# A two-layer graph network kernel: gather in plain f32, one summed row-norm operand, other first loads, another order of the last pair

## The chip, the cores and the metric

The kernel runs on one core of a Trainium2 chip. The metric is the device time of one execution in microseconds (us), 1934.1 as the median of three runs (1933.42 to 1934.23). In the profile PE is TensorE (matmuls), PEld its loading of weights, DVE is VectorE, ACT is ScalarE, POOL is GpSimd and SP is SyncE, which here only starts transfers.

## The reference

There are 64 graphs of 256 nodes with 512 features, one adjacency matrix of 256 x 256 zeros and ones for all, and two layers:

```python
# layer 0
h = relu(layernorm(x))
q, k, v = h @ Wq.T, h @ Wk.T, h @ Wv.T
rel = adj.T * (q @ k.T)
rel = rel / norm(rel, axis=2)           # length of each row
x = x + rel @ v
# layer 1
h = relu(layernorm(x))
x = x + (adj @ h) @ weight + bias
```

All of it is float32.

## The kernel before

**Tiling.** The graphs are taken two at a time, as 32 pairs. A pair is a tile `x` of 128 partitions by 2 graphs by 2 halves of the nodes by 512 features (1 MB). Layer 0 folds Wq and Wk into one matrix, `m_sb`, made at the start (L346 to L355), so that only `g` (`project_g`) and `v` (`project_v`) are computed per pair. These two and layer 1's product with `weight` (`mix`) use a Winograd form of the 2 x 2 block product: seven block products instead of eight (`winograd`, L137), each of four matmuls, accumulated in three PSUM banks `bank_a`, `bank_c` and `bank_b` and taken out between them by ACT copies (first write) or DVE additions. Their left sums come from `left_sums` on DVE.

**Stages of pair i.** `ln0` normalizes x and applies the relu (statistics on DVE, the relu as four ACT instructions, L200). `transposes` turns h on TensorE through one PSUM bank, copied out by ACT. `scores` makes rel (L260), multiplies it with adj on DVE and squares it on ACT into `sq` (L265). `attend` computes rel @ v (L275) and the row norms: for each 128 rows two matmuls of `sq`, one for each half of the other node index, with a column of ones, added up in the bank `pn` (L285). ACT and DVE then turn `pn` into 1/norm (L290, L291) and DVE adds to x (L293). `ln1` normalizes the new x, applies the relu, and adds the bias to x on POOL (L309). `gather` is adj @ h2 (L323). `gather_sums` and `mix` finish layer 1, and the pair goes out in one transfer from POOL (L343).

**Two forms of gather.** At the start the kernel looks at the low 12 bits of all entries of adj (L372 to L383). If any is set, it runs the loop over the pairs with `gather` as plain f32 matmuls. If none is set (zeros and ones have none), it runs a second copy of the loop in which h2 is written as a sum of two fp32r terms `h2s`: ACT casts each of the four chunks (L204), DVE subtracts the cast from the original (L205), and `gather` multiplies both terms with `adjt_r`, an fp32r copy of adj transposed. A value read into registers and a branch (L421 to L426) choose the copy; nothing of a branch mixes with what stands before it.

**Order.** The loop over pairs is software-pipelined by hand: scores(i), sums of gather(i-1), transposes(i+1), mix(i-1), attend(i), project_g(i+1), ln1(i), project_v(i+1), ln0(i+2), gather(i). The order of the text is a rank. The framework's planner places each engine's instructions ahead of time by that rank and by its own estimate of when each is ready, adds the waits, and hands out buffers; each engine then works through its list in that fixed order. So an instruction of lower rank may be placed ahead of one of higher rank where the planner sees a gap.

**Loads.** SP starts the loads of x, three pairs ahead (L80). The first x has a buffer of its own, the others share four. ACT starts Wq, Wk and Wv in this order, POOL starts adj, `weight` and the bias.

Of the kernel before, what the change touches and what calls it, by code (L numbers as in the profile page):

```python
# [8 lines left out]

F32 = mybir.dt.float32  # L10
F32R = mybir.dt.float32r
I32 = mybir.dt.int32
AF = mybir.ActivationFunctionType
ALU = mybir.AluOpType
EPS = 1e-5
# [3 lines left out]
def kernel(  # L19
# [22 lines left out]

    nc = tc.nc
    P = 128
    B, N, D = x.shape
# [11 lines left out]
    outs = out.rearrange("(i b) (c p) d -> i p b c d", b=NB, p=P)  # L65

    const = ctx.enter_context(tc.tile_pool(name="const", bufs=1))
    xpool = ctx.enter_context(tc.tile_pool(name="xpool", bufs=4))
    work = ctx.enter_context(tc.tile_pool(name="work", bufs=1))
    small = ctx.enter_context(tc.tile_pool(name="small", bufs=3))  # L70
    ps_t = ctx.enter_context(tc.tile_pool(name="ps_t", bufs=1, space=bass.MemoryType.PSUM))
# [3 lines left out]
    X, H, HT, HS, G, V, R, H2, Y, YS = ({} for _ in range(10))  # L75

    def load(i):
        pool, tag = (const, "x_first") if i == 0 else (xpool, "x")
        X[i] = pool.tile([P, NB, NC, D], F32, tag=tag, name=f"x_{i}")
        nc.sync.dma_start(out=X[i], in_=xs[i])  # L80


    load(0)
    ident = const.tile([P, P], F32, name="ident")
    make_identity(nc, ident)
    ones = const.tile([P, 1], F32, name="ones")
    nc.gpsimd.memset(ones, 1.0)

    wq_sb = work.tile([P, DC, D], F32, tag="g", name="wq_sb")
    wk_sb = work.tile([P, DC, D], F32, tag="v", name="wk_sb")  # L90
    wv_sb = work.tile([P, DC, D], F32, tag="yt", name="wv_sb")
    nc.scalar.dma_start(out=wq_sb, in_=wq.rearrange("(c p) d -> p c d", p=P))
    nc.scalar.dma_start(out=wk_sb, in_=wk.rearrange("(c p) d -> p c d", p=P))
    nc.scalar.dma_start(out=wv_sb, in_=wv.rearrange("(c p) d -> p c d", p=P))
    adj_sb = const.tile([P, NC, N], F32, name="adj_sb")
    nc.gpsimd.dma_start(out=adj_sb, in_=adj.rearrange("(c p) n -> p c n", p=P))
    w_sb = const.tile([P, DC, D], F32, name="w_sb")
    nc.gpsimd.dma_start(out=w_sb, in_=weight.rearrange("(c p) d -> p c d", p=P))
    bias_bc = const.tile([P, D], F32, name="bias_bc")
    nc.gpsimd.dma_start(  # L100
        out=bias_bc, in_=bass.AP(tensor=bias.tensor, offset=bias.offset, ap=[[0, P], [1, D]])
# [78 lines left out]
        return product  # L180


    def norm_relu(dst, src, split=None):

        st = small.tile([P, TC, 6], F32, tag="st", name="st")
        mv = small.tile([P, TC, 2], F32, tag="mv", name="mv")
        rs = small.tile([P, TC], F32, tag="rs", name="rs")  # L190
        nb = small.tile([P, TC], F32, tag="nb", name="nb")
        for c in range(TC):
            nc.vector.bn_stats(st[:, c, :], src[:, c, :])  # L193
            nc.vector.bn_aggr(mv[:, c, :], st[:, c, :])  # L194
        nc.vector.tensor_scalar(rs, mv[:, :, 1], 0.0, EPS, op0=ALU.max, op1=ALU.add)
        nc.scalar.activation(rs, rs, AF.Sqrt)
        nc.vector.reciprocal(rs, rs)
        nc.vector.scalar_tensor_tensor(nb, mv[:, :, 0], -1.0, rs, op0=ALU.mult, op1=ALU.mult)
        for c in range(TC):
            nc.scalar.activation(  # L200
                dst[:, c, :], src[:, c, :], AF.Relu, bias=nb[:, c : c + 1], scale=rs[:, c : c + 1]
            )
            if split is not None:
                nc.scalar.copy(split[:, 0, c, :], dst[:, c, :])  # L204
                nc.vector.tensor_sub(split[:, 1, c, :], dst[:, c, :], split[:, 0, c, :].bitcast(F32))  # L205


    def ln0(i):
        pool, tag = (const, "h_first") if i == 0 else (work, "h")
        H[i] = pool.tile([P, TC, D], F32, tag=tag, name=f"h_{i}")  # L210
        norm_relu(H[i], flat(X[i]))

    def transposes(i):
        h = H.pop(i)
# [37 lines left out]
    def scores(i):  # L252
        ht, g = HT.pop(i), G.pop(i).rearrange("p e h (b n) -> p e h b n", b=NB)
        rel = work.tile([P, NB, NC, N], F32, tag="rel", name=f"rel_{i}")
        sq = work.tile([P, NB, NC, N], F32, tag="sq", name=f"sq_{i}")
        for b in range(NB):
            pm = ps_m.tile([P, NC, N], F32, tag="pm", name="prel")
            for m in range(NC):
                for e in range(DC):
                    nc.tensor.matmul(  # L260
                        pm[:, m, :], ht[:, e, m, ts(b, P)], g[:, e, :, b, :],
                        start=(e == 0), stop=(e == DC - 1),
                    )
            nc.vector.tensor_mul(rel[:, b], pm, adj_sb)  # L264
            nc.scalar.activation(sq[:, b], rel[:, b], AF.Square)  # L265
        R[i] = (rel, sq)

    def attend(i):
        (rel, sq), v, xt = R.pop(i), flat(V.pop(i)), flat(X[i])
        pu = []  # L270
        for b in range(NB):
            for n in range(NC):
# [8 lines left out]
        for b in range(NB):  # L281
            for n in range(NC):
                c = b * NC + n
                for m in range(NC):
                    nc.tensor.matmul(  # L285
                        pn[:, c : c + 1], sq[:, b, m, ts(n, P)], ones,
                        start=(m == 0), stop=(m == NC - 1),
                    )
        rn = small.tile([P, TC], F32, tag="rn", name="rn")
        nc.scalar.activation(rn, pn, AF.Sqrt)  # L290
        nc.vector.reciprocal(rn, rn)  # L291
# [4 lines left out]
            )  # L296


    def ln1(i, exact):
        h2 = work.tile([P, TC, D], F32, tag="h2", name=f"h2_{i}")  # L300
        xt = flat(X[i])
        if exact:
            H2[i] = work.tile([P, 2, TC, D], F32R, tag="h2s", name=f"h2s_{i}")
            norm_relu(h2, xt, split=H2[i])
        else:
            H2[i] = h2
            norm_relu(h2, xt)
        for c in range(TC):
            nc.gpsimd.tensor_tensor(xt[:, c, :], xt[:, c, :], bias_bc, ALU.add)  # L309

    def gather(i, exact):
        h2 = H2.pop(i)
        if exact:
            terms = [(h2[:, s], adjt_r[:, m, :], m) for m in range(NC) for s in range(2)]
        else:
            terms = [(h2, adjt_sb[:, m, :], m) for m in range(NC)]
        Y[i] = work.tile([P, DC, NC, NB, P], F32, tag="yt", name=f"yt_{i}")
        for b in range(NB):
            for d0 in range(0, DC, 2):
                pm = ps_m.tile([P, 2, N], F32, tag="pm", name="py")  # L320
                for d in range(2):
                    for n, (left, right, m) in enumerate(terms):
                        nc.tensor.matmul(  # L323
                            pm[:, d, :], left[:, b * NC + m, ts(d0 + d, P)], right,
                            start=(n == 0), stop=(n == len(terms) - 1),
                        )
                nc.scalar.copy(
                    Y[i][:, d0 : d0 + 2, :, b, :], pm.rearrange("p d (h n) -> p d h n", h=NC)
                )
        Y[i] = Y[i].rearrange("p d h b n -> p d h (b n)")  # L330
# [4 lines left out]
    def mix(i):  # L335
# [4 lines left out]
            nc.vector.tensor_add(dst, bank.rearrange("p (b e) -> p b e", b=NB), dst)  # L340

        winograd(product_weights_moving(left_operands(Y.pop(i), YS.pop(i)), w_right), take)
        nc.gpsimd.dma_start(out=outs[i], in_=xt)  # L343


    m_sb = const.tile([P, DC, D], F32, name="m_sb")  # L346
# [18 lines left out]
    for m in range(NC):  # L365
# [3 lines left out]
    w_right = right_operands(w_sb, "w")  # L369


    adjt_r = const.tile([P, NC, N], F32R, name="adjt_r")  # L372
    nc.vector.tensor_copy(adjt_r, adjt_sb)
    low = const.tile([P, NC * N], I32, name="low")
    nc.vector.tensor_single_scalar(
        low, adj_sb.rearrange("p c n -> p (c n)").bitcast(I32), 0xFFF, op=ALU.bitwise_and
    )
    low_max = const.tile([P, 1], F32, name="low_max")
    nc.vector.tensor_reduce(low_max, low, axis=mybir.AxisListType.X, op=ALU.max)
    pf = ps_m.tile([P, 512], F32, tag="pm", name="pf")  # L380
    nc.tensor.matmul(pf[0:1, 0:1], low_max, ones, start=True, stop=True)
    low_any = const.tile([1, 1], I32, name="low_any")
    nc.vector.tensor_copy(low_any, pf[0:1, 0:1])  # L383


    ln0(0)

    def pairs(exact):
        for j in (1, 2):
            if j < NP:  # L390
                load(j)
        transposes(0)
        project_g(0)
        project_v(0)
        if NP > 1:
            ln0(1)
        for i in range(NP):
            nxt = i + 1 < NP
            if i + 3 < NP:
                load(i + 3)  # L400
            scores(i)
            if i > 0:
                gather_sums(i - 1)
            if nxt:
                transposes(i + 1)
            if i > 0:
                mix(i - 1)
            attend(i)
            if nxt:
                project_g(i + 1)  # L410
            ln1(i, exact)
            if nxt:
                project_v(i + 1)
            if i + 2 < NP:
                ln0(i + 2)
            gather(i, exact)
        gather_sums(NP - 1)
        mix(NP - 1)

    first = X[0], H[0]  # L420
    inexact = nc.values_load(low_any[0:1, 0:1], min_val=0, max_val=P * 0xFFF)  # L421
    with tc.If(inexact > 0) as either:
        pairs(False)
    X[0], H[0] = first
    with either.Else():
        pairs(True)  # L426


# [26 lines left out]
```

## Time and profile before

| | us |
|---|---|
| median of three runs | 1934.1 |
| the profiled execution's own time | 1934.1 |
| its span, first to last recorded event | 1932.3 |
| PE busy | 1876.4 |
| PEld busy | 1540.2 |
| DVE busy | 952.9 |
| ACT busy | 599.9 |
| POOL busy | 230.6 |

A line of the costliest groups gives the line of the source, the engine and operation, what is written from what, shapes and type, and the number of instructions; after the bar the busy time of the group in us and the mean of one in ns; after the second bar how long the engine was idle just before them, and what ended most of that. A line of the order of time gives start and length in us, engine, line, operation, and in brackets a wait ahead of it. Matmuls are pipelined and their ends are modelled, so the recorded lengths of neighbours overlap; the distance between the starts of two stages is the safer measure. In the chain of waits, "issue" is time in which the engine waited for nothing that the profile shows.

### The profile page before, as it was taken

How to read it: one execution, taken by the hardware profiler on the slowest of the kernel's cores; microseconds unless marked ns; L12 is line 12 of the kernel's file. 1: busy time of each engine (PE TensorE's matmuls, PEld its weight loads, DVE VectorE, ACT ScalarE, POOL GpSimd, SP SyncE). 2: the span in 40 equal slices, each digit the busy share in tenths (PEclk: the TensorE clock that was granted, in tenths of full speed). 3: DMA queues.
4: the chain of work that ended last, by engine and by line, in shares of the span. 5: the costliest groups of instructions: out<-in, count | busy, mean ns of one | idle time of the engine just before them, and what ended most of it. 6: DMA issues, size and time to landing. Idle time of an engine off the chain costs nothing.

```text
span 1932.3 us, 21628 instructions
## 1 busy us (share of the span) xinstructions
PE 1876.4 (97%) x9014; PEld 1540.2 (80%) x9014; DVE 952.9 (49%) x1744; ACT 599.9 (31%) x1066; POOL 230.6 (12%) x170
## 2 busy tenths in 40 slices
PE   4999999999999999999999999999999999999996
PEld 2788878888878888878888888888888888788885
DVE  2355554455554454554455554454554454554444
ACT  2233332233332333332333322333322333322321
POOL 0011110011110111110111110111110111110111
PEclk8999999999999999999999999999999999999998
DMA  5000111101111101111101111001111001110001
GB/s 174 35 13 10 44 44 44 44 1 44 44 44 44 44 1 44 44 44 44 37 8 44 44 44 44 24 21 44 44 44 44 22 23 44 44 44 23 10 13 44
DMA packets 27721, 73.28 MB, mean 38 GB/s; under 512 B 1120, under 2 KB 1120, under 8 KB 27616
## 3 DMA queue, kind: packets, MB, share of 16 engines
q1 hardware_dynamic: 16896, 33.56, 5.3%
q0 software_dynamic: 9136, 35.13, 4.8%
q10 hardware_dynamic: 1584, 3.15, 0.4%
q8 instruction: 72, 1.18, 0.2%
q14 instruction: 33, 0.27, 0.0%
HBM read 38.27 MB, written 33.55 MB: 37 GB/s over the span
## 4 chain that ended last, share of the span: by engine, by line
PE 66%; DVE 21%; ACT 11%; DMA 1%; issue 1%; DVEq 0%; POOLq 0%; ACTq 0%
PE bank_a L175 18%; PE prel L260 11%; PE pu L275 11%; DVE st L193 7%; ACT h L200 7%; PE py L323 6%; PE bank_c L175 6%; PE bank_b L175 5%; DVE h2s L205 4%; DVE x L293 4%; PE pt L220 3%; PE pn L285 3%; ACT h2s L204 2%; DVE g L235 2%; DVE mv L194 1%; PE pw L350 1%
## 5 line engine op out<-in xcount | busy, mean ns | idle before, releaser
L309 POOL TENSOR_TENSOR x<-x,bias_bc 128x512 f32<-128x512 f32 x128 | 203.0, 1614 | 630.8 <-ACT h L200 617.2
L200 ACT ACTIVATE h<-x,nb,rs 128x512 f32<-128x512 f32 x256 | 194.3, 807 | 105.8 <-DVE mv L194 55.0
L260 PE MATMUL prel<-g,ht 128*128 128x256 f32 x1024 | 226.2, 379 | 0.0
L275 PE MATMUL pu<-v,rel 128*128 128x512 f32 x512 | 225.4, 592 | 0.0
L260 PEld LDWEIGHTS prel<-g,ht 128*128 128x128 f32 x1024 | 192.1, 190 | 24.9
L205 DVE TENSOR_TENSOR h2s<-h,h2s 128x512 fp32r<-128x512 f32 x128 | 165.7, 1334 | 46.8 <-ACT h2s L204 46.7
L275 PEld LDWEIGHTS pu<-v,rel 128*128 128x128 f32 x512 | 97.0, 190 | 107.3 <-issue 105.7
L290 ACT ACTIVATE rn<-pn 128x4 f32<-128x4 f32 x32 | 5.6, 174 | 548.4 <-PE pn L285 548.4
L193 DVE BATCH_NORM_STATS2 st<-x 128x6 f32<-128x512 f32 x256 | 167.1, 665 | 0.8 <-DMA x<-in_x_dram 0.8
L343 POOL DMA_DIRECT2D out_dram<-x x32 | 24.7, 772 | 1064.6 <-DVE x L340 928.8
L323 PE MATMUL py<-adjt_r,h2s 128*128 128x256 f32 x1024 | 133.9, 289 | 9.7 <-ACT h2s L204 9.0
L175 PE MATMUL bank_a<-wv_t,hs 128*128 128x256 f32 x512 | 127.2, 391 | 12.6 <-ACT v L246 12.6
L323 PEld LDWEIGHTS py<-adjt_r,h2s 128*128 128x128 f32 x1024 | 126.5, 192 | 12.2 <-ACT h2s L204 9.1
L291 DVE RECIPROCAL rn<-rn 128x4 f32<-128x4 f32 x32 | 5.7, 178 | 253.2 <-ACT rn L290 253.2
L175 PEld LDWEIGHTS bank_a<-wv_t,hs 128*128 128x128 f32 x512 | 92.3, 189 | 45.5 <-ACT v L246 35.4
L340 DVE TENSOR_TENSOR x<-bank_a,x 128x512 f32<-128x512 f32 x128 | 88.0, 687 | 69.3 <-PE bank_a L175 69.3
L163 PE MATMUL bank_a<-hs,m_t 128*128 128x256 f32 x512 | 121.0, 379 | 0.0
L175 PE MATMUL bank_a<-w_t,ys 128*128 128x256 f32 x512 | 121.0, 379 | 0.0
L223 ACT COPY ht<-pt 128x512 f32<-128x512 f32 x128 | 75.0, 586 | 143.4 <-PE pt L220 143.4
L163 PEld LDWEIGHTS bank_a<-hs,m_t 128*128 128x128 f32 x512 | 97.2, 190 | 13.3 <-ACT g L233 0.2
L175 PEld LDWEIGHTS bank_a<-w_t,ys 128*128 128x128 f32 x512 | 97.3, 190 | 13.2
L264 DVE TENSOR_TENSOR rel<-prel,adj_sb 128x512 f32<-128x512 f32 x64 | 44.3, 692 | 114.3 <-PE prel L260 114.3
(101 smaller groups left out, 2830.3 us busy)
## 6 DMA issues: line engine op xcount, KB each, us to landing
x<-in_x_dram SPq DMA_DIRECT2D x32, 1024.0 KB, 5.5
out_dram<-x POOLq DMA_DIRECT2D x32, 1024.0 KB, 4.7
wq_sb<-in_L_gnn_Wq_dram ACTq DMA_DIRECT2D x1, 1024.0 KB, 11.7
wk_sb<-in_L_gnn_Wk_dram ACTq DMA_DIRECT2D x1, 1024.0 KB, 15.1
wv_sb<-in_L_gnn_Wv_dram ACTq DMA_DIRECT2D x1, 1024.0 KB, 17.1
w_sb<-in_L_gnn_weight_dram POOLq DMA_DIRECT2D x1, 1024.0 KB, 10.7
adj_sb<-in_adj_dram POOLq DMA_DIRECT2D x1, 256.0 KB, 7.4
bias_bc<-in_L_gnn_bias_dram POOLq DMA_DIRECT2D x1, 256.0 KB, 11.0
```

What stands on the lines that cost most here:

```text
L163: nc.tensor.matmul(bank[:, e * HT_ : (e + 1) * HT_], right[n][:, d, ts(e, P)], left[n][:, d, :], start=(start and e == 0 and d == 0), stop ...
L175: nc.tensor.matmul(bank[:, b * HD : (b + 1) * HD], left[n][:, d, ts(b, P)], right[n][:, d, :], start=(start and b == 0 and d == 0), stop=( ...
L193: nc.vector.bn_stats(st[:, c, :], src[:, c, :])
L200: nc.scalar.activation(dst[:, c, :], src[:, c, :], AF.Relu, bias=nb[:, c : c + 1], scale=rs[:, c : c + 1])
L205: nc.vector.tensor_sub(split[:, 1, c, :], dst[:, c, :], split[:, 0, c, :].bitcast(F32))
L223: nc.scalar.copy(HT[i][:, d].rearrange("p h t -> p (h t)"), pt)
L260: nc.tensor.matmul(pm[:, m, :], ht[:, e, m, ts(b, P)], g[:, e, :, b, :], start=(e == 0), stop=(e == DC - 1),)
L275: nc.tensor.matmul(pm[:, :D], rel[:, b, m, ts(n, P)], v[:, b * NC + m, :], start=(m == 0), stop=(m == NC - 1),)
L293: nc.vector.scalar_tensor_tensor(xt[:, c, :], pu[c][:, :D], rn[:, c : c + 1], xt[:, c, :], op0=ALU.mult, op1=ALU.add,)
L309: nc.gpsimd.tensor_tensor(xt[:, c, :], xt[:, c, :], bias_bc, ALU.add)
L323: nc.tensor.matmul(pm[:, d, :], left[:, b * NC + m, ts(d0 + d, P)], right, start=(n == 0), stop=(n == len(terms) - 1),)
L340: nc.vector.tensor_add(dst, bank.rearrange("p (b e) -> p b e", b=NB), dst)
```

## The change

- The look at adj's low bits, the branch and the copy of the loop with fp32r terms go. One loop remains, with `gather` as f32 matmuls of h2 and `adjt_sb`.
- In `scores`, POOL adds the squares of the two halves into a new tile `sqs`; in `attend` one matmul for each 128 rows takes the place of two.
- First loads: Wq goes first on SP, then x_0, behind it the other x; ACT starts Wk, Wv and `weight`; POOL starts adj and the bias. x_0 comes from the shared buffers, now five, and h_0 from the shared one.
- `norm_relu` is split into `norm` (statistics, scale and shift) and `relu`. In layer 1 `norm` keeps its place ahead of project_v(i+1), and `relu` with the bias additions comes after it.
- In the last pair, mix(30) comes after attend(31) and norm(31), ahead of the relu. The last pair's output is started on SP in two transfers, one for each half of the nodes.

```diff
-    xpool = ctx.enter_context(tc.tile_pool(name="xpool", bufs=4))
+    xpool = ctx.enter_context(tc.tile_pool(name="xpool", bufs=5))
...
+    nc.sync.dma_start(out=wq_sb, in_=wq.rearrange("(c p) d -> p c d", p=P))
+    nc.scalar.dma_start(out=wk_sb, in_=wk.rearrange("(c p) d -> p c d", p=P))
     load(0)
+    nc.scalar.dma_start(out=wv_sb, in_=wv.rearrange("(c p) d -> p c d", p=P))
...
-    nc.gpsimd.dma_start(out=w_sb, in_=weight.rearrange("(c p) d -> p c d", p=P))
+    nc.scalar.dma_start(out=w_sb, in_=weight.rearrange("(c p) d -> p c d", p=P))
...
+        sqs = work.tile([P, NB, N], F32, tag="sqs", name=f"sqs_{i}")
+        nc.gpsimd.tensor_tensor(sqs, sq[:, :, 0], sq[:, :, 1], ALU.add)
+        R[i] = (rel, sqs)
...
-                for m in range(NC):
-                    nc.tensor.matmul(
-                        pn[:, c : c + 1], sq[:, b, m, ts(n, P)], ones,
-                        start=(m == 0), stop=(m == NC - 1),
-                    )
+                nc.tensor.matmul(pn[:, c : c + 1], sqs[:, b, ts(n, P)], ones, start=True, stop=True)
...
-                    for n, (left, right, m) in enumerate(terms):
+                    for m in range(NC):
                         nc.tensor.matmul(
-                            pm[:, d, :], left[:, b * NC + m, ts(d0 + d, P)], right,
-                            start=(n == 0), stop=(n == len(terms) - 1),
+                            pm[:, d, :], h2[:, b * NC + m, ts(d0 + d, P)], adjt_sb[:, m, :],
+                            start=(m == 0), stop=(m == NC - 1),
                         )
...
-        nc.gpsimd.dma_start(out=outs[i], in_=xt)
+        if i + 1 < NP:
+            nc.gpsimd.dma_start(out=outs[i], in_=xt)
+        else:
+            for t in range(NC):
+                nc.sync.dma_start(out=outs[i][:, :, t], in_=xt[:, :, t])
...
+        if i > 0 and nxt:
+            mix(i - 1)
+        attend(i)
+        if nxt:
+            project_g(i + 1)
+        scale_shift = norm(flat(X[i]))
+        if nxt:
+            project_v(i + 1)
+        else:
+            mix(i - 1)
+        ln1_relu(i, scale_shift)
+        if i + 2 < NP:
+            ln0(i + 2)
+        gather(i)
...
-    inexact = nc.values_load(low_any[0:1, 0:1], min_val=0, max_val=P * 0xFFF)
-    with tc.If(inexact > 0) as either:
-        pairs(False)
-    X[0], H[0] = first
-    with either.Else():
-        pairs(True)
```

More of the change, by code (lines that the diff above doesn't have):

```diff
@@ L10 @@
 F32 = mybir.dt.float32
-F32R = mybir.dt.float32r
-I32 = mybir.dt.int32
 AF = mybir.ActivationFunctionType
@@ L77, in load @@
     def load(i):
-        pool, tag = (const, "x_first") if i == 0 else (xpool, "x")
-        X[i] = pool.tile([P, NB, NC, D], F32, tag=tag, name=f"x_{i}")
+        X[i] = xpool.tile([P, NB, NC, D], F32, tag="x", name=f"x_{i}")
         nc.sync.dma_start(out=X[i], in_=xs[i])
+    wq_sb = work.tile([P, DC, D], F32, tag="g", name="wq_sb")
+    wk_sb = work.tile([P, DC, D], F32, tag="v", name="wk_sb")
+    wv_sb = work.tile([P, DC, D], F32, tag="yt", name="wv_sb")
+    nc.sync.dma_start(out=wq_sb, in_=wq.rearrange("(c p) d -> p c d", p=P))
+    nc.scalar.dma_start(out=wk_sb, in_=wk.rearrange("(c p) d -> p c d", p=P))
     load(0)
+    nc.scalar.dma_start(out=wv_sb, in_=wv.rearrange("(c p) d -> p c d", p=P))
     ident = const.tile([P, P], F32, name="ident")
@@ L87 @@
     nc.gpsimd.memset(ones, 1.0)
[L89 to L94, printed above, removed]
     adj_sb = const.tile([P, NC, N], F32, name="adj_sb")
@@ L180, in product_weights_moving, with norm @@
         return product
-    def norm_relu(dst, src, split=None):
+    def norm(src):
         st = small.tile([P, TC, 6], F32, tag="st", name="st")
@@ L198, in norm_relu, with relu @@
         nc.vector.scalar_tensor_tensor(nb, mv[:, :, 0], -1.0, rs, op0=ALU.mult, op1=ALU.mult)
+        return rs, nb
+    def relu(dst, src, scale_shift):
+        rs, nb = scale_shift
         for c in range(TC):
@@ L202, in norm_relu @@
             )
-            if split is not None:
-                nc.scalar.copy(split[:, 0, c, :], dst[:, c, :])
-                nc.vector.tensor_sub(split[:, 1, c, :], dst[:, c, :], split[:, 0, c, :].bitcast(F32))
     def ln0(i):
-        pool, tag = (const, "h_first") if i == 0 else (work, "h")
-        H[i] = pool.tile([P, TC, D], F32, tag=tag, name=f"h_{i}")
-        norm_relu(H[i], flat(X[i]))
+        H[i] = work.tile([P, TC, D], F32, tag="h", name=f"h_{i}")
+        relu(H[i], flat(X[i]), norm(flat(X[i])))
     def transposes(i):
@@ L265, in scores @@
             nc.scalar.activation(sq[:, b], rel[:, b], AF.Square)
-        R[i] = (rel, sq)
+        sqs = work.tile([P, NB, N], F32, tag="sqs", name=f"sqs_{i}")
+        nc.gpsimd.tensor_tensor(sqs, sq[:, :, 0], sq[:, :, 1], ALU.add)
+        R[i] = (rel, sqs)
     def attend(i):
-        (rel, sq), v, xt = R.pop(i), flat(V.pop(i)), flat(X[i])
+        (rel, sqs), v, xt = R.pop(i), flat(V.pop(i)), flat(X[i])
         pu = []
@@ L296, in attend, with ln1_relu, gather @@
             )
-    def ln1(i, exact):
-        h2 = work.tile([P, TC, D], F32, tag="h2", name=f"h2_{i}")
+    def ln1_relu(i, scale_shift):
+        H2[i] = work.tile([P, TC, D], F32, tag="h2", name=f"h2_{i}")
         xt = flat(X[i])
[L302 to L307, printed above, removed]
+        relu(H2[i], xt, scale_shift)
         for c in range(TC):
             nc.gpsimd.tensor_tensor(xt[:, c, :], xt[:, c, :], bias_bc, ALU.add)
-    def gather(i, exact):
+    def gather(i):
         h2 = H2.pop(i)
[L313 to L316, printed above, removed]
         Y[i] = work.tile([P, DC, NC, NB, P], F32, tag="yt", name=f"yt_{i}")
@@ L369 @@
     w_right = right_operands(w_sb, "w")
[L372 to L380, printed above, removed]
@@ L381 @@
-    nc.tensor.matmul(pf[0:1, 0:1], low_max, ones, start=True, stop=True)
-    low_any = const.tile([1, 1], I32, name="low_any")
-    nc.vector.tensor_copy(low_any, pf[0:1, 0:1])
-    ln0(0)
[L388 to L418, printed above, removed]
@@ L420 @@
-    first = X[0], H[0]
-    inexact = nc.values_load(low_any[0:1, 0:1], min_val=0, max_val=P * 0xFFF)
-    with tc.If(inexact > 0) as either:
-        pairs(False)
-    X[0], H[0] = first
-    with either.Else():
-        pairs(True)
+    ln0(0)
+    for j in (1, 2):
+        if j < NP:
+            load(j)
+    transposes(0)
+    project_g(0)
+    project_v(0)
+    if NP > 1:
+        ln0(1)
+    for i in range(NP):
+        nxt = i + 1 < NP
+        if i + 3 < NP:
+            load(i + 3)
+        scores(i)
+        if i > 0:
+            gather_sums(i - 1)
+        if nxt:
+            transposes(i + 1)
+        if i > 0 and nxt:
[4 more added lines that the diff above has]
+        scale_shift = norm(flat(X[i]))
+        if nxt:
+            project_v(i + 1)
[5 more added lines that the diff above has]
+        gather(i)
@@ L430 @@
+    gather_sums(NP - 1)
+    mix(NP - 1)
 _INS = ["x", "adj", "L0_gnn_Wq", "L0_gnn_Wk", "L0_gnn_Wv", "L1_gnn_weight", "L1_gnn_bias"]
```

## The prediction

> **What bounds the kernel now.** I read the page first, its costliest groups, then the order of time in one steady pair, then the chain of waits at the start, then TensorE alone at the end. The page says TensorE is the bound and shows the rate of each kind of matmul:
>
> ```profile
> PE 1876.4 (97%) x9014; PEld 1540.2 (80%) x9014; DVE 952.9 (49%) x1744; ACT 599.9 (31%) x1066; POOL 230.6 (12%) x170
> ...
> L260 PE MATMUL prel<-g,ht 128*128 128x256 f32 x1024 | 226.2, 379 | 0.0
> ...
> L205 DVE TENSOR_TENSOR h2s<-h,h2s 128x512 fp32r<-128x512 f32 x128 | 165.7, 1334 | 46.8 <-ACT h2s L204 46.7
> ...
> L323 PE MATMUL py<-adjt_r,h2s 128*128 128x256 f32 x1024 | 133.9, 289 | 9.7 <-ACT h2s L204 9.0
> ```
>
> Scores (L260) are written as 16 matmuls per pair and gather (L323) as 32, yet both show 1024 records: an f32 matmul is two instructions, an fp32r one is one. For 1024 instructions of 256 columns the f32 group is busy 226.2 us, the fp32r group 133.9. So the kernel took the branch that splits h2 in two fp32r terms, and there the gather is cheap on TensorE. Starts of one steady pair, in order of time (start, length, engine):
>
> ```profile
> 918.78 1.89 PE L175 MATMUL bank_a<-wvt_sb,ht 128*128 128x256 f32 x8
> ...
> 926.93 1.99 PE L175 MATMUL bank_a<-wv_t,hs 128*128 128x256 f32 x8 [0.43 <-ACT v L246]
> ...
> 931.60 4.00 PE L323 MATMUL py<-adjt_r,h2s 128*128 128x256 f32 x32
> ...
> 935.44 7.07 PE L260 MATMUL prel<-g,ht 128*128 128x256 f32 x32
> ...
> 942.35 0.60 PE L220 MATMUL pt<-ident,h 128*128 128x128 f32 x4
> ...
> 963.14 1.84 PE L285 MATMUL pn<-ones,sq 128*128 128x1 f32 x16
> ...
> 964.84 0.46 PE L163 MATMUL bank_a<-ht,m_sb 128*128 128x256 f32 x1
> ```
>
> Lengths overlap, so I price a stage by the distance between starts. Gather: 935.44-931.60 = 3.84 (3.90 as a mean of 31 pairs, same reading). Scores, also 32 instructions: 6.91. Row norms: 1.70. The v stage: 12.82, where the same stage without layer 1 beside it (pair 0, starts 61.33 and 73.42) takes 12.09; two waits for v copies (L246) make up the rest. One pair is 58.29 us, of which about 0.8 is idle. TensorE otherwise waits only at the two ends. The start, from the chain of waits:
>
> ```profile
> 1.27 15.06 DMA wk_sb<-in_L_gnn_Wk_dram
> 16.48 16.26 PE pw L350 x32
> ...
> 38.08 5.01 issue
> ...
> 43.09 1.13 PE pt L220 x4
> ```
>
> TensorE begins when wk lands, and after the last matmul on adj's bits (34.84) does nothing until 43.09: value, registers, branch. The end, TensorE alone:
>
> ```profile
> 1874.56 1.89 PE L175 MATMUL bank_a<-w_sb,yt 128*128 128x256 f32 x8
> ...
> 1893.51 1.84 PE L285 MATMUL pn<-ones,sq 128*128 128x1 f32 x16
> 1904.34 1.73 PE L323 MATMUL py<-adjt_r,h2s 128*128 128x256 f32 x5 [8.99 <-ACT h2s L204]
> 1906.76 6.04 PE L323 MATMUL py<-adjt_r,h2s 128*128 128x256 f32 x27 [0.68 <-DVE h2s L205]
> ...
> 1912.64 1.89 PE L175 MATMUL bank_a<-w_sb,yt 128*128 128x256 f32 x8
> ```
>
> After pair 31's row norms nothing covers layer 1's normalization: 8.99 us idle, and the gather then limps behind the split for 8.30 us.
>
> **What the Trainium skill says.** FP8 and Floating Point Precision, TensorE Precision Notes: true FP32 needs four passes through the array, reduced-precision FP32 reads four bytes and truncates. The trace agrees in direction: 6.91 us for 16 f32 matmuls, 3.90 for 32 fp32r ones, so 432 against 122 ns each, and two fp32r terms still cost 244. SBUF — State Buffer, SBUF: two separate sides: a DVE operation with two SBUF inputs and a GpSimd operation that reads SBUF exclude each other. The trace agrees: L205 runs beside the bias adds (L309) and takes 1334 ns, left sums of the same size 692. DMA: Bandwidth & Descriptors, Queues, rings and completion order: each DMA engine takes the queues in turn, packet by packet; the first loads here share like that (x_0, alone on its queue, is in by 10.7, wk, second on its own, at 16.34). Runtime: NRT & Kernel Launch, Instruction fetch mechanics: a taken branch may have to fetch its target; the 5.01 us "issue" after the bits is such a gap, though the trace does not split it.
>
> **The change part by part**, against the profiled execution's span of 1932.3 us.
>
> *Gather in f32.* Removing the branch removes the split too: 16 f32 matmuls on h2 and adjt_sb, 32 instructions of the form of L260. Price 6.91 instead of 3.90: +3.01 a pair, 31 pairs: **+93.3** (the last is counted below). L260 is the same shape and type in every pair, so the bounds are narrow, +92 to +95. What goes with the split, 71.9 us of casts (L204) and 165.7 us of subtractions (L205), lies on engines that are 31% and 49% busy; it is worth only the waits below.
>
> *Row norms.* Half the matmuls: 8 instructions instead of 16, 0.85 instead of 1.70, 31 times: **-26.4** (-24 to -28). The new add on POOL is the form of L309, 1.6 us (1.28 to 1.76). In the steady pair its second input (sq of L265) ends at 944.1 and the norms start at 963.14: 19 us hide it. In the last pair, with mix moved away, scores end and 6.87 us of attention follow; sq ends about 1.5 us in, the sum 1.6 later, so 3.5 us are left. Were the cover gone, it would be 1.6 us a pair, 51 us. On POOL it stands ahead of the output DMA's wait and behind the bias adds, which end at 924.0; beside it run left sums on DVE, which may take 1.3 instead of 0.7 with over a microsecond to spare.
>
> *Relu behind v copies.* The two waits in the v stage are 12.81-12.09 = 0.72 us in 30 pairs, 21.6 in all. First, at 922.15, a v copy stands behind two relus and two casts; second, at 926.32, behind a relu that waited for nb, which waited for DVE, held until 924.57 by L205. Casts and subtractions disappear and the v copies rank first. A single relu (0.81) before a copy (0.59) fits in the 1.72 us until the bank is wanted. Bounds 0 and -21.6 (the instruction order is planned, so a relu may still stand badly); I take **-18**. Behind the later relus stand the bias adds on POOL: they have until mix of the next pair, some 15 us.
>
> *Start.* wk moves to the head of ACT's queue, wq to SP's ahead of x_0. On the old order a queue's first megabyte lands at 10.7 (x_0) to 12.4 us (wq, 0.74+11.7), with three queues sharing; POOL's loses w, so less shares. Until 16.48 some 317 GB/s were moved; wq, wk and POOL's 0.5 MB make 2.6 MB, 8.3 us at that rate, and about 1.3 us before it: 9.5. Saved 7.0 (4 to 8). x_0 lands by some 15, h at some 22, transposes want it at 28; wv and w by 20, wanted at 26 or hidden. The branch gap from 34.84 to 43.09: 8.25 saved, all of it, since h is ready. TensorE then has not cooled, transposes come at 1.33 us as in the loop and not 1.79: 1.2 saved. Sum **-16.5** (-12 to -20).
>
> *Last pair and end.* From the end of scores (1874.56) 57.74 us remained. New: attention 6.87 + norms 0.85 + mix of pair 30 12.08 (it covers the 8.6 us that first relus need after the norms, plus three or four of mix's own 0.69 us additions on DVE) + f32 gather 6.91 + mix 12.08 + last addition 0.9 + half an output. The 1 MB output was issued at 1926.17 and the span ended 6.1 later; half of it is sent a product earlier, on SP, whose loads are long done: some 5.6. Sum 45.3: **-12.4** (-10 to -14).
>
> The fifth buffer of x replaces the separate first one; loads wait longer on SP than anyone waits for them (DVE waited for x 0.8 us once), so 0.
>
> Sum: 93.3-26.4-18-16.5-12.4 = +20.0, a span of 1952.3. The profiled execution took 1934.1 with 1.8 around its span, and 1934.1 is also the median of the three runs: **1954 us**.
>
> **Rivals.**
> - *The v waits stay.* For it: the order on ACT is fixed by a planner, and the relus of ln0 still wait for DVE. Against: all that filled ACT and DVE there is gone, and the last pair, with fewer relus, already shows 11.89. It gives 1954+18 = 1972.
> - *A new wait takes its place.* Ranked behind the v copies, the first two relu chunks might end after the last v copy; gather follows the v stage at once on TensorE. Against: nb is known at 916.5, 15 us before gather. Two relus and a copy late, 0.76x2+0.59+0.2 = 2.3 us a pair, give +71: 2025. One late gives about 1980.
> - *Not slower*: the f32 gather runs faster than scores. Only this can offset the rest, since at 6.91 the pair's bare work grows from 57.44 to 59.6. At the old 117 to 122 ns per instruction the sum gives 1954-32x3.01 = 1858; as the change costs 20.0 us and gather has 32x32 instructions, it decides from 215.9-20000/1024 = 196 ns down. Nothing in the trace has an f32 instruction of 256 columns at that pace.
> - *The start gives less* (x_0 or wv late): inside the bounds, up to +7.
>
> **How the numbers follow.** Likeliest case 0.69, its own range 1946 to 1963 from the bounds of head, end and v waits; v waits stay 0.17; new wait 0.11; f32 gather fast 0.03. To leave no more than two in ten out, the range goes from 1944 to 1976: it holds the first and most of the second. Within 0.2% (3.9 us, about what a measurement tells from no change) and faster come only from the last rival: faster 0.02, same 0.01, slower 0.97.
>
> **What would show it.** In the profile after: L323's line as f32, 1024 records at about 221 us busy; distance from its start to that of scores 6.9; pn x256 and 0.85 between starts; v stage 12.1 to 12.3; TensorE starting near 9.5 and no gap before the first transposes; no idle over 1 us between norms and gather of the last pair; a pair of about 59.8 us instead of 58.29. Wrong would be: a "py <- ACT h" wait in each pair, a "pn <- POOL sqs" wait, or a first transposes that wait for x_0.

## The result: 1979.7 us, slower by 2.4%, and the profile after

The changed kernel takes 1979.72 us (median of four runs), the kernel before 1933.76 beside it: 1.0239 times as long, with an interval of 1.0221 to 1.0257. The forecast was 1954 in a range of 1944 to 1976, so the direction was right and the size was not: 46.0 us lost where 20 were foreseen. The profiled spans differ by 1978.1-1932.3 = 45.8 us, which is what the table below adds up to.

The page of the changed kernel, engines and the groups that answer to those shown of before:

```profile
PE 1946.2 (98%) x8756; PEld 1583.9 (80%) x8756; DVE 823.2 (42%) x1612; ACT 534.0 (27%) x939; POOL 224.9 (11%) x200
...
L303 PE MATMUL py<-adjt_sb,h 128*128 128x256 f32 x1024 | 226.4, 379 | 0.0
L251 PE MATMUL prel<-g,ht 128*128 128x256 f32 x1024 | 226.2, 379 | 0.0
...
L166 PE MATMUL bank_a<-wv_t,hs 128*128 128x256 f32 x512 | 124.1, 385 | 11.4 <-ACT v L237 11.4
```

Gather (L303) now costs what scores (L251) cost, 226.4 against 226.2 us busy, where the fp32r gather took 133.9. DVE lost 130 us of work and ACT 66, and it bought nothing: the wait of the v stage for v copies, 12.6 us in the profile before, still stands there with 11.4.

The order of time over the v stage of one steady pair (start, length, engine, line; in brackets the wait ahead of it):

```profile
935.95 0.15 DVE L189 SCALAR_TENSOR_TENSOR nb<-mv,rs 128x4 f32<-128x4 f32 x1
...
936.13 2.93 ACT L195 ACTIVATE h<-x,nb,rs 128x512 f32<-128x512 f32 x4 [1.83 <-DVE nb L189]
...
937.04 4.95 POOL L293 TENSOR_TENSOR x<-x,bias_bc 128x512 f32<-128x512 f32 x4 [16.46 <-ACT h L195]
938.20 1.89 PE L166 MATMUL bank_a<-wvt_sb,ht 128*128 128x256 f32 x8
938.97 0.56 ACT L224 COPY g<-bank_a 128x512 f32<-128x512 f32 x1
939.43 0.20 ACT L187 ACTIVATE rs<-rs 128x4 f32<-128x4 f32 x1
939.67 0.18 DVE L188 RECIPROCAL rs<-rs 128x4 f32<-128x4 f32 x1 [2.30 <-ACT rs L187]
939.88 0.90 DVE L189 SCALAR_TENSOR_TENSOR nb<-mv,rs 128x4 f32<-128x4 f32 x1
...
940.86 0.81 ACT L195 ACTIVATE h<-x,nb,rs 128x512 f32<-128x512 f32 x1 [1.23 <-issue]
941.58 0.56 ACT L237 COPY v<-bank_a 128x512 f32<-128x512 f32 x1
942.05 1.52 ACT L195 ACTIVATE h<-x,nb,rs 128x512 f32<-128x512 f32 x2
942.20 1.99 PE L166 MATMUL bank_a<-wv_t,hs 128*128 128x256 f32 x8 [0.38 <-ACT v L237]
943.47 0.57 ACT L237 COPY v<-bank_c 128x512 f32<-128x512 f32 x1
```

Read it backwards. TensorE wants bank_a at about 941.6 and gets it at 942.20, after the copy at 941.58 (the product before it started at 939.93 and takes 1.72). The stage's first product had filled the bank 1.5 us ahead of that copy, but the copy stands on ACT behind the relu of 940.86. That relu belongs to ln0, two pairs ahead. It waits for its shift nb, an operation of four elements a partition that took 0.15 us at 935.95 and takes 0.90 at 939.88, in the middle of POOL's four bias additions. (That the additions cause this is shown further down, by without_bias and nb_one_input.) Layer 1's own relu, which the change ranks behind the v copies, had run in one piece at 936.13, ahead of them all.

Where the 45.8 us are, as distances between starts in both traces:

| stretch | before | after | in all | forecast |
|---|---|---|---|---|
| start to the first scores | 73.42 | 61.97 | -11.45 | -16.5 |
| gather, 31 pairs | 3.90 | 6.91 | +93.0 | +93.3 |
| row norms, 31 pairs | 1.70 | 0.81 | -27.6 | -26.4 |
| v stage, 30 pairs | 12.81 | 12.89 | +2.5 | -18 |
| transposes and mix, 30 pairs | 13.93 | 13.99 | +1.7 | 0 |
| from the last scores to the end | 64.65 | 52.21 | -12.4 | -12.4 |

A steady pair takes 60.54 us, 58.29 before. The start, in the order of time:

```profile
0.74 0.49 ACTq L78 DMA_DIRECT2D wk_sb<-in_L_gnn_Wk_dram  x1
...
0.75 0.43 SPq L77 DMA_DIRECT2D wq_sb<-in_L_gnn_Wq_dram  x1
...
12.29 16.90 PE L334 MATMUL pw<-wk_sb,wq_sb 128*128 128x512 f32 x32 [12.29 <-DMA wk_sb<-in_L_gnn_Wk_dram]
16.46 1.28 DVE L184 BATCH_NORM_STATS2 st<-x 128x6 f32<-128x512 f32 x2 [16.46 <-DMA x<-in_x_dram]
...
31.21 0.60 PE L211 MATMUL pt<-ident,h 128*128 128x128 f32 x4
...
33.42 0.66 PE L211 MATMUL pt<-ident,h 128*128 128x128 f32 x4 [1.61 <-ACT ht L214]
```

The gap at the branch is gone (the first transposes follow at 31.21, before at 43.09), but wk lands at 12.24 and not at 9.5, and the second set of transposes waits 1.61 us for a copy that stands on ACT behind those of Wv and adj.

### The profile page after: what moved, and what is told of

Read it like the earlier page. It is cut to its first block, busy times and chain, and to the rows that moved or that the text cites. A ratio compares the mean times of both kernels' runs of the same rounds, so it can differ in the third digit from the quotient of the medians.

```text
span 1978.1 us, 21025 instructions
## 1 busy us (share of the span) xinstructions
PE 1946.2 (98%) x8756; PEld 1583.9 (80%) x8756; DVE 823.2 (42%) x1612; ACT 534.0 (27%) x939; POOL 224.9 (11%) x200
## 5 line engine op out<-in xcount | busy, mean ns | idle before, releaser
L303 PE MATMUL py<-adjt_sb,h 128*128 128x256 f32 x1024 | 226.4, 379 | 0.0
L251 PE MATMUL prel<-g,ht 128*128 128x256 f32 x1024 | 226.2, 379 | 0.0
L293 POOL TENSOR_TENSOR x<-x,bias_bc 128x512 f32<-128x512 f32 x128 | 158.3, 1264 | 521.6 <-ACT h L195 508.3
L303 PEld LDWEIGHTS py<-adjt_sb,h 128*128 128x128 f32 x1024 | 194.6, 190 | 26.5
L251 PEld LDWEIGHTS prel<-g,ht 128*128 128x128 f32 x1024 | 194.6, 190 | 26.4
L184 DVE BATCH_NORM_STATS2 st<-x 128x6 f32<-128x512 f32 x256 | 167.0, 664 | 16.5 <-DMA x<-in_x_dram 16.5
L258 POOL TENSOR_TENSOR sqs<-sq 128x512 f32<-128x512 f32 x32 | 40.6, 1269 | 840.5 <-issue 772.9
L166 PE MATMUL bank_a<-wv_t,hs 128*128 128x256 f32 x512 | 124.1, 385 | 11.4 <-ACT v L237 11.4
L307 ACT COPY yt<-py 128x512 f32<-128x512 f32 x128 | 75.0, 586 | 149.4 <-PE py L303 149.4
L120 DVE TENSOR_TENSOR ys<-yt 128x512 f32<-128x512 f32 x32 | 22.2, 693 | 216.0 <-ACT yt L307 216.0
L237 ACT COPY v<-bank_a 128x512 f32<-128x512 f32 x96 | 55.1, 574 | 199.6 <-PE bank_a L166 199.6
```

The costliest lines, as they stand in the source:

```text
L166: nc.tensor.matmul(bank[:, b * HD : (b + 1) * HD], left[n][:, d, ts(b, P)], right[n][:, d, :], start=(start and b == 0 and d == 0), stop=( ...
L237: nc.scalar.copy(dst, src)
L251: nc.tensor.matmul(pm[:, m, :], ht[:, e, m, ts(b, P)], g[:, e, :, b, :], start=(e == 0), stop=(e == DC - 1),)
L303: nc.tensor.matmul(pm[:, d, :], h2[:, b * NC + m, ts(d0 + d, P)], adjt_sb[:, m, :], start=(m == 0), stop=(m == NC - 1),)
L307: nc.scalar.copy(Y[i][:, d0 : d0 + 2, :, b, :], pm.rearrange("p d (h n) -> p d h n", h=NC))
```

## The experiments

**Theories.** A: the v waits come from the place of ln0's relus in ACT's fixed order, ahead of v copies. B: that place does harm only because the shift nb of these relus is late, held on DVE by POOL's bias additions. C: layer 1's relus, the ones that the change ranks anew, make or cure the waits. Further runs do single parts of the change alone.

**relu_first.** Layer 1's relu goes back ahead of project_v.

```diff
         if nxt:
+            ln1_relu(i, scale_shift)
             project_v(i + 1)
         else:
             mix(i - 1)
-        ln1_relu(i, scale_shift)
+            ln1_relu(i, scale_shift)
```

> The changed kernel with layer 1's relu back ahead of project_v, as it stood before. Theory A (the v waits of 0.8 us a pair come from the relus of ln0(i+2) that stand ahead of the v copies in ACT's fixed order; ranking layer 1's relu behind the v copies moves nothing): the v stage stays at 12.89 us and the time within 2 us of 1979.7. Theory C (layer 1's relus are what the rank acts on): the v stage changes by 0.3 us or more a pair, the time by 9 us or more.

Measured: 1979.33 us (ratio to before 1.0230, 1.0213 to 1.0247), v stage 12.89. This part of the change does nothing: layer 1's relu is ready some 4 us before the first v copy can start, and the planner places it there at either rank. In the two profiles every engine works through the same list in the same order, the 939 instructions of ACT and the 8756 of TensorE among them. So the rank moved nothing; but since nothing moved, this run says nothing of what these relus would do in another place. C is answered by the next two runs, where the waits go although layer 1's relus stay.

**ln0_early.** ln0 of two pairs ahead follows transposes directly.

```diff
         if nxt:
             transposes(i + 1)
+        if i + 2 < NP:
+            ln0(i + 2)
...
         ln1_relu(i, scale_shift)
-        if i + 2 < NP:
-            ln0(i + 2)
         gather(i)
```

> The changed kernel with ln0(i+2) directly after transposes(i+1) and no longer after project_v, so that its four relus fall into the stretch where ACT has little to do. Theory A (the relus of ln0 ahead of the v copies) and theory B (the same relus, but only because their shift nb is held up on DVE by the bias additions on POOL): v stage 12.1 to 12.2 instead of 12.89, about 0.75 x 30 = 22 us less, 1957. Theory C (the four relus of layer 1 in a row before the last g copy): unchanged, 1979 to 1980.

Measured: 1958.33 us (1.0121, 1.0105 to 1.0138), v stage 12.09, its bare work. In the order of time of this kernel, a steady pair:

```profile
929.26 4.94 POOL L293 TENSOR_TENSOR x<-x,bias_bc 128x512 f32<-128x512 f32 x4 [16.46 <-ACT h L195]
...
932.11 0.89 DVE L189 SCALAR_TENSOR_TENSOR nb<-mv,rs 128x4 f32<-128x4 f32 x1
...
932.40 0.59 ACT L237 COPY v<-bank_a 128x512 f32<-128x512 f32 x1 [0.54 <-PE bank_a L166]
```

A shift is still held for 0.89 us beside POOL, but the relu that needs it now runs some 29 us later, and the v copy starts as soon as its bank is full. The start is 3.2 us longer here (first scores at 65.21 instead of 61.97; the second set of transposes waits 4.37 us for a copy on ACT); the loop gains more. This fits A and B. C falls: layer 1's four relus still run in one piece ahead of the v copies, from 928.36 on.

**without_bias.** The bias additions are left out, and with them the bias in the output.

```diff
-        for c in range(TC):
-            nc.gpsimd.tensor_tensor(xt[:, c, :], xt[:, c, :], bias_bc, ALU.add)
```

> The changed kernel without the bias additions on POOL; the output lacks the bias. Everything else keeps its place. Theory B (POOL's additions hold nb of ln0 on DVE, 0.90 us where it takes 0.16, and so the relu and the v copy behind it): the first v copy comes in time, the v stage falls to 12.1 to 12.3, the time to about 1960. Theory A (the place of the relus alone): v stage above 12.7, the time within 5 us of 1979.7.

Measured: 1956.57 us (1.0115, 1.0098 to 1.0132), v stage 12.17. The lists of ACT, DVE and TensorE are those of the changed kernel, instruction by instruction and in the same order, relu ahead of copy; only POOL has its 128 bias additions less:

```profile
928.42 0.16 DVE L189 SCALAR_TENSOR_TENSOR nb<-mv,rs 128x4 f32<-128x4 f32 x1
...
928.67 0.81 ACT L195 ACTIVATE h<-x,nb,rs 128x512 f32<-128x512 f32 x1 [0.49 <-ACT rs L187]
929.39 0.56 ACT L237 COPY v<-bank_a 128x512 f32<-128x512 f32 x1
929.85 1.52 ACT L195 ACTIVATE h<-x,nb,rs 128x512 f32<-128x512 f32 x2
930.00 1.68 PEld L166 LDWEIGHTS bank_a<-wv_t,hs 128*128 128x128 f32 x8
930.19 1.89 PE L166 MATMUL bank_a<-wv_t,hs 128*128 128x256 f32 x8
```

With nb at its 0.16 us the relu starts 0.7 us earlier against the stage's start, and the first v copy, without having moved, is done by the time TensorE wants the bank. Of the 23.2 us gained, the v stage gives 21.6 and the start 1.2. A alone falls, B holds.

**nb_one_input.** The same with the bias kept: the shift is computed so that no instruction reads two tensors.

```diff
-        nc.vector.scalar_tensor_tensor(nb, mv[:, :, 0], -1.0, rs, op0=ALU.mult, op1=ALU.mult)
+        for c in range(TC):
+            nc.vector.tensor_scalar(nb[:, c : c + 1], mv[:, c, 0:1], rs[:, c : c + 1], -1.0, op0=ALU.mult, op1=ALU.mult)
```

> The changed kernel with the shift nb made by four small DVE instructions that read one tensor and a scalar for each partition, in place of one that reads two tensors; the bias additions stay on POOL, the result is the same. Theory B in its sharp form (POOL's addition holds only DVE instructions with two tensors from SBUF): none of the four takes over 0.2 us, the v stage falls from 12.89 to 12.1 to 12.4, the time to 1957 to 1965. If any DVE instruction is held while POOL adds: one of the four still takes some 0.9 us, v stage 12.9 or more, 1980 or more.

Measured: 1956.94 us (1.0119, 1.0102 to 1.0136), v stage 12.11. The groups of nb, by shape (busy us, mean ns after the bar), first in the changed kernel:

```profile
L189 DVE SCALAR_TENSOR_TENSOR nb<-mv,rs 128x4 f32<-128x4 f32 x64 | 31.9, 499 | 1.1
```

and, in this kernel:

```profile
L190 DVE TENSOR_SCALAR nb<-mv,rs 128x1 f32<-128x1 f32 x256 | 36.6, 205 | 1.2
```

One instruction of 499 ns in the mean (30 of the 64, those beside POOL's additions, take some 0.9 us, the others 0.15 to 0.16) against four of 205 that are never held (201 to 215 ns, though 120 of the 256 run beside a POOL addition). The four together are not less work, but the first relu chunk needs only the first of them. The Trainium skill states this in SBUF — State Buffer, Who interferes with whom: a DVE instruction with two inputs from SBUF contends with a GpSimd instruction that reads SBUF, one with at most one does not, as long as it is outside the modes that use two ports; and in DVE: scalar operands, raw-bit mode, write accounting and state across instructions, 1. Scalar operands: a scalar for each partition does not take up the second tensor stream. The runs agree on both: two inputs were held at four elements a partition, and a tensor with a scalar, at one element, was not. The planner put one relu fewer between the two v copies here, so the place helped a little too; without_bias shows that it isn't needed.

**f32_gather_alone.** The kernel before, its two branches swapped.

```diff
     with tc.If(inexact > 0) as either:
-        pairs(False)
+        pairs(True)
...
     with either.Else():
-        pairs(True)
+        pairs(False)
```

> The kernel before with only its two branches swapped: zeros and ones now take the plain f32 gather; the look at adj, the registers and the branch stay. The gather costs 3.00 us more in 31 pairs, +93; the last pair gains about 2.5 without the split. If casts and subtractions of the split made the v waits, 0.72 x 30 = 21.6 go: 2003. If they did not, 2024.

Measured: 2031.28 us (1.0499, 1.0481 to 1.0516), 7 above the higher expectation. The v stage is 12.90: casts and subtractions, which stood in the way of the v copies before, are gone, and the held nb is in the way at once, 502 ns in the mean against 157:

```profile
965.14 0.89 DVE L198 SCALAR_TENSOR_TENSOR nb<-mv,rs 128x4 f32<-128x4 f32 x1
...
966.12 0.81 ACT L200 ACTIVATE h<-x,nb,rs 128x512 f32<-128x512 f32 x1 [1.22 <-issue]
966.84 0.56 ACT L246 COPY v<-bank_a 128x512 f32<-128x512 f32 x1
```

Between first and last scores 97.8 us are lost and not 93: the v stage 0.09 and transposes with mix 0.06 a pair longer. The end gains 0.9 and not 2.5; its gather comes after 7.78 us of idle TensorE and takes 8.67 us where the loop's takes 6.91. The profile also gives the clock granted to TensorE, as a share of its full speed: 0.50 from 1994.2 to 2004.4, which takes in the first 3.4 us of this gather, and 1.00 after it. At half speed 3.4 us do the work of 1.7, so by this estimate the clock makes up 1.7 of the 1.76 us. So this one part costs 97 us; all others together return 52.

**sum_alone.** The kernel before with the squares summed on POOL.

```diff
-        R[i] = (rel, sq)
+        sqs = work.tile([P, NB, N], F32, tag="sqs", name=f"sqs_{i}")
+        nc.gpsimd.tensor_tensor(sqs, sq[:, :, 0], sq[:, :, 1], ALU.add)
+        R[i] = (rel, sqs)
```

(and the one matmul of the change in place of two.)

> The kernel before with only the squares added on POOL and half the row-norm matmuls. In the changed kernel the distance from these matmuls to the next stage is 0.81 us, before it is 1.70: 0.89 x 32 = 28.5 less, 1905. If the addition on POOL holds up left sums on DVE that mix waits for, some of it comes back: 1907 with the 0.06 us a pair by which transposes and mix are longer in the changed kernel; no gain at all would mean that the matmuls wait for the sum.

Measured: 1905.44 us (0.9856, 0.9841 to 0.9871). Row norms 0.81, transposes and mix 13.93 as before: the sum is wholly hidden, and the 0.06 a pair of the changed kernel is not its doing, since the f32 gather alone shows it. What makes it there stays open.

**loads_alone.** The kernel before with the change's order of first loads on SP, ACT and POOL.

```diff
+    nc.sync.dma_start(out=wq_sb, in_=wq.rearrange("(c p) d -> p c d", p=P))
+    nc.scalar.dma_start(out=wk_sb, in_=wk.rearrange("(c p) d -> p c d", p=P))
     load(0)
+    nc.scalar.dma_start(out=wv_sb, in_=wv.rearrange("(c p) d -> p c d", p=P))
...
-    nc.gpsimd.dma_start(out=w_sb, in_=weight.rearrange("(c p) d -> p c d", p=P))
+    nc.scalar.dma_start(out=w_sb, in_=weight.rearrange("(c p) d -> p c d", p=P))
```

> The kernel before with only the new order of the first loads. In the changed kernel the first matmuls start at 12.29 instead of 16.48: 4.2 us less, 1929.8. If they start earlier without anything behind them moving up (x_0, wv or w then being late), nothing: 1934.

Measured: 1929.87 us (0.9984, 0.9977 to 0.9990). TensorE starts at 12.91 and the first scores move from 73.42 to 70.65, so 2.8 us reach the loop and not 4.2. The kernel before took 1933.5 us beside this run, and not 1934.1; that the time expected is met this closely is luck.

**after_split.** The changed kernel with the two fp32r terms back, and neither look nor branch; it is exact only for an adj such as this one.

```diff
-                    for m in range(NC):
+                    for n, (left, right, m) in enumerate(terms):
                         nc.tensor.matmul(
-                            pm[:, d, :], h2[:, b * NC + m, ts(d0 + d, P)], adjt_sb[:, m, :],
-                            start=(m == 0), stop=(m == NC - 1),
+                            pm[:, d, :], left[:, b * NC + m, ts(d0 + d, P)], right,
+                            start=(n == 0), stop=(n == len(terms) - 1),
```

(with the casts and subtractions of before in `relu`.)

> The changed kernel with the gather in two fp32r terms, without look or branch (it is then exact only for an adj like the one here, zeros and ones). Gather 3.90 instead of 6.91 us in 31 pairs, -93; the last pair about 1 us either way. If the v stage stays as it is, 1979.7 - 94 = 1886. If the casts and subtractions add waits, up to 1890; if they only take the place of the present ones, 1886.

Measured: 1878.44 us (0.9717, 0.9702 to 0.9731), 8 us better than expected. Gather takes 4.02 and the v stage 12.59: here the planner put v copies between relus and casts, and part of the waits went (9 us in 30 pairs; start and end give 3 more, the gather takes some back). The change with the gather of before, and without the look, is thus a gain of 55 us.

**best.** The kernel before, with its look, branch and fp32r gather, and with the sum on POOL, the new loads, the last pair's order and output, and ln0 directly after transposes.

```diff
             if nxt:
                 transposes(i + 1)
+            if i + 2 < NP:
+                ln0(i + 2)
-            if i > 0:
+            if i > 0 and nxt:
                 mix(i - 1)
```

(with the edits of sum_alone and loads_alone, and the change's last pair.)

> The kernel before, with its look, branch and fp32r gather, and with: the squares added on POOL, the new loads, the last pair's order and output of the changed kernel, and ln0(i+2) directly after transposes(i+1). From the parts: row norms -28.5, loads -4.2, last pair -14, v waits -21.6 if ln0's relus make them both, -11 if layer 1's casts keep the first of the two: 1866 to 1877.

Measured: 1867.08 us (0.9659, 0.9645 to 0.9674), 3.4% under the kernel before. A pair takes 56.68 us, the v stage 12.12, the end from the last scores 50.72.

## Why the prediction was wrong

- **Gather and row norms: right.** +3.00 and -0.89 a pair against +3.01 and -0.85. Pricing by the row of the same shape and type (scores) was sound.
- **Relu behind v copies: wrong, and the main miss.** The step of the prediction said that casts and subtractions disappear and the v copies then rank first, -18. It measured +2.5, 20.5 of the 25.8 us missed. Two things in it failed. "The v copies rank first" took a rank in the text for a place on ACT; relu_first shows that the rank moved nothing. And removing L205 was taken to remove the lateness of nb, but L205 had only come first. Before the change nb started when POOL's additions were done (924.0) and took 0.16 us:

```profile
921.76 2.81 DVE L205 TENSOR_TENSOR h2s<-h,h2s 128x512 fp32r<-128x512 f32 x2 [0.56 <-ACT h2s L204]
...
924.69 0.16 DVE L198 SCALAR_TENSOR_TENSOR nb<-mv,rs 128x4 f32<-128x4 f32 x1
...
924.89 1.52 ACT L200 ACTIVATE h<-x,nb,rs 128x512 f32<-128x512 f32 x2 [1.57 <-DVE nb L198]
926.32 0.56 ACT L246 COPY v<-bank_a 128x512 f32<-128x512 f32 x1
```

With L205 gone nb comes while POOL still adds, and the additions hold nb itself, 0.90 us. The rule was in the prediction, applied to L205 beside L309, and not to the other instruction with two tensors in the same window. The rival "the v waits stay" was the case that came true, with 0.17; its 1972 falls 8 short, mainly for the start.
- **Start: right parts, sizes off by 5.0 us.** -11.45 lies outside the bounds of -12 to -20, and three sizes were wrong. First, wk was taken to land at 9.5, from 2.6 MB at 317 GB/s, and landed at 12.24 (2.7 us). The rate was right and the bytes were not: by 12.24 the DMA engines had moved 3.4 MB, for which the prediction's own sum, 1.3 us and then 317 GB/s, gives 12.1. By queue, SP's had moved 1.58 MB and ACT's 1.33, so 0.5 MB of x and 0.3 MB of Wv went ahead of the end of wk, and the sum had neither. Second, the first matmuls took 16.74 between starts and not 16.08 (0.7): a few at their head come every 0.85 us instead of 0.43, and this cost 3.0 us in all and not 2.3. Third, the transposes stage did not get 1.2 shorter but 0.4 longer (1.6). Its second set waits 1.61 us on ACT, behind the copies of Wv and adj that the gap at the branch had covered. And the clock, which was to stay up without that gap, fell to 0.50 here too, from 35.2 to 38.6 (before: from 38.1 to 48.4): the last two sets stand 2.20 us apart and not 1.33. In without_bias, where the profile has no such stretch, they stand 1.36 apart.
- **Last pair and end: right in the sum, partly by luck.** -12.4 was foreseen and measured.

```profile
1940.48 1.97 PE L166 MATMUL bank_a<-w_sb,yt 128*128 128x256 f32 x8
...
1947.07 1.99 PE L166 MATMUL bank_a<-w_t,ys 128*128 128x256 f32 x8 [1.17 <-DVE x L320]
...
1955.13 6.21 PE L303 MATMUL py<-adjt_sb,h 128*128 128x256 f32 x28
...
1971.54 1.89 PE L166 MATMUL bank_a<-w_t,yt 128*128 128x256 f32 x8
```

The two mixes and the gather were put at 31.1 us and take 32.8 (from 1940.48 to 1.72 us past the last start), mostly because mix of pair 30 waits 1.17 us for an addition queued on DVE behind the statistics; part of the gather is placed inside mix. What follows was put at 6.5 us and takes 4.8, as half an output lands in less time than was thought. The two misses cancel. One reading of the kernel before was wrong too: it put the 8.30 us of the last gather down to the split. The granted clock there is 0.50 from 1898.4 to 1912.0, nearly to the end of that gather; as an estimate, its work of 3.90 us at that clock and the wait of 0.68 make up the 8.30 within some 0.3. In the changed kernel TensorE stands idle there for no more than 1.17 us, and the clock is 1.00 from 38.6 to 1977.4.
- **The signs.** Of what the likeliest case was to show, "v stage 12.1 to 12.3", "no idle over 1 us" in the last pair and "TensorE starting near 9.5" did not come (12.89, 1.17 and 12.29). None of the signs named as wrong came either: the gather waits for no relu, the row norms for no sum, and the first transposes not for x_0. The v stage's length was the only sign that pointed at the main miss.

## What to carry to other kernels

A stall that ends with a slow instruction may have a second cause waiting behind it: before counting its removal as a gain, look at what else runs beside the late instruction in the same window, and at what that shares with the engine that is late. A rank in the program is a gain only if it moves an instruction on its engine; look whether the one to be outranked is ready before the other anyway. A shift that reads two tensors from SBUF can cost five times its price beside a GpSimd operation, and one rewritten with a scalar operand does not. Where TensorE has stood idle, look at the granted clock before you blame the work behind the gap.

## What the runs showed of the hardware that was not expected

- A DVE instruction of four elements a partition with two tensors from SBUF was held for the rest of a POOL addition of 1.26 us: 0.90 us instead of 0.16, in 30 of 64 cases, each ending within 0.03 us of the addition. With the shift rewritten so that no instruction reads two tensors, the kernel took 23 us less. DVE additions of 512 elements that read one bank of PSUM and one tensor of SBUF (to `g`) took 0.69 us beside POOL's additions, as elsewhere.
- TensorE was granted half of its clock for some 3.4 to 13.7 us at a time: in the kernel before around the gap at the branch and around the idle stretch of the last pair. The gather behind it took 8.30 us instead of 3.90 there, and in f32_gather_alone 8.67 instead of 6.91.
- Wq and Wk, 1 MB each, first on SP's and ACT's queue and started within 10 ns of each other, landed 2.5 us apart (9.75 and 12.24). By 3.0 us SP's queue had moved 0.17 MB and ACT's nothing; from 4 to 9 us both moved the same, 0.70 and 0.73 MB, so ACT's stayed behind. In loads_alone the two queues start just so, yet the loads landed 1.0 us apart. Why ACT's queue starts later, and why the distance differs, is open; the other way round was not tried.
- The gap around the branch, 8.25 us from the last matmul before it to the first after, is gone when the branch goes, but the copies on ACT that it had covered then cost 1.61 us of waiting.
